# Re-laid timetables and a re-dealt GpSimd share in a two-layer kNN-attention and Mamba kernel

## The chip, the cores and the metric

The kernel runs on one core of one Trainium2 chip. The metric is the device time of one execution in microseconds (us). A core has five engines that run side by side, each working through its own instructions in order: PE (TensorE, matrix products), DVE (VectorE, here the scans and elementwise work), ACT (ScalarE, activations and copies), POOL (GpSimd, here two kinds of products) and SP (SyncE, which issues the DMAs). They wait for each other through semaphores. Tiles lie in SBUF or, for matmul results and the decays, in PSUM.

## What is computed

The input is x, 8 images of 256 channels and 48 x 48 = 2304 tokens, in float32. Two residual layers follow each other:

```python
# layer 0: groupnorm, then kNN attention over the 2304 tokens of an image
feat_pos = tokens @ W.T + bias            # 256 feature and 256 position channels
pos = pos / max(norm(pos), 1e-12)
sim = pos @ pos.T
topksim, topkid = top_k(sim, 16)
x = x + sum_k softmax(topksim)[k] * feat[topkid[k]]

# layer 1: groupnorm, then two Mamba blocks, one on top of the other (DEPTH = 2)
xn = layernorm(xf)                        # over channels
xi, z = split(xn @ in_w.T)                # 512 each
xc = silu(causal_conv4(xi))
dt_r, Bm, Cm = split(xc @ xp_w.T)         # 16 each
dt = softplus(dt_r @ dtp_w.T + dtp_b)
h = h * exp(dt * A) + dt * Bm * xc        # 512 channels x 16 states, step by step in time
y = (h * Cm).sum(states) + xc * D
out = (y * silu(z)) @ out_w.T
x = x + (both blocks)
```

## The kernel before

**Units.** The tokens of an image are cut into six chunks of 384. One *unit* is one chunk in one of the two Mamba blocks, so an image has 12 units, and there are 96. Within an image they run in a fixed order, numbered 0 to 11 ("at" in the code), so that a chunk's second block follows its first by a few units. A unit has 16 *steps*, each for 32 channels with their 16 states, as 128 partitions by four states along the tile; a step has two *halves* of two states each. So a unit has 32 *positions* (HOOKS), and the kernel has 3072 half steps, numbered m.

**What a half step does.** For each step POOL makes the input of the recurrence, B times dt x, into a tile `bx` (L893, "making"), two steps ahead. ACT computes the decays exp(dt A) of a half (L917) into one of two PSUM banks, `da`, from the tile `dtr`, which a DMA fills with the step's dt (`load_rep`, L626 to L641). `dtr` has three fixed buffers, the one for step n being number n modulo 3. DVE runs the recurrence over time as a scan (L932). Then h is multiplied by C. This *C product* is dealt out by a letter of the string SHARE: with G the scan writes into `bx` and POOL multiplies later (`pool_part`, L960, both halves of a step in one instruction if both are G); with V the scan writes into its bank `da`, DVE multiplies at once (L934) and ACT copies the carried state from the bank (L948). After every four steps PE sums the states (`sum_states k`, L975 and L978, into y_k), which frees four of the eight `bx` tiles.

**Three tables.** The units are in one of three stages, each with a SHARE string and a timetable of its own: stage 0 for units 1 to 9 of images 0 to 6 (63 units), where the next image's layer-0 top-k runs in between; stage 1 for units 0, 10 and 11 of these images (21 units, the "spare" tables); stage 2 for the last image (12 units).

**The order of the work** is written out by hand; no scheduler reorders it. The loop at the end of the program goes through the half steps, and each engine executes in the order in which the instructions are emitted:

```python
for m in range(first, PARTS * NSTEP - HOOKS + last + 1):
    carry(m - 1); decay(m + 1)
    if p == 0:
        make_bx(n + LEAD); pool_part(n - 1); take_up(n + 1)
    else:
        carry_pool(n - 1)
    # the items of the inner table at m   ("between")
    run_scan(m)
    # the items of the outer table at m   ("behind")
    # one piece of the next image's layer 0
```

An item is a position and a function. Position -20 means 20 half steps before the unit's own start (so position 12 of the unit before), 33 means position 1 of the unit after. Items at the same position run in the order of the list. A unit's own preparation thus lies in the units ahead of it: load_v, the layernorm (center, square, variance, root, spread_root, which gives lb, and scale at L750), weight loads `load_in e` (L653, four buffers `inw`) and `in_proj e` (L686, e = 0 to 7), `tap e` (L774 to L784, on ACT) and `taps e` (L791, on DVE) of the convolution, silu_x (table loads L797 and L800 around L799), x_proj, step_size (L821), softplus (table load L827), times_x (L841 and the stores at L844), and the loads `load_rep dt i` and `load_rep dtx i` of step i. After the steps follow sum_states, gate (L984), out_proj (L996) and leave. `load_d k` (L773) loads the matrix that adds D times xc in sum_states k. In the next image's layer 0, L324 to L372 and L444 to L539 are the normalised positions, similarities, top-k and attention.

Of the kernel before, what the change touches and what calls it, by code (L numbers as in the profile page):

```python
# [26 lines left out]
def tile_conv_preact(  # L27
# [46 lines left out]


    SHARE = (
        "GGVGGGVGGGVVGGVGGGGVGGGVGGGGGVVG",
        "GVGGGVVVGGVVGGGVVGGGVGVVGGVVGVGV",
        "VVVGVVGGGVVVGGVVGGGVGGVVVVGGGVVG",
    )  # L80
    assert N % T == 0 and N % P == 0 and T % P == 0 and NS % (J * HQ) == 0

# [770 lines left out]
    def silu_z(unit):  # L853
# [3 lines left out]
        for e in range(DB - 1):  # L857
# [11 lines left out]
             dt=[], dt_d={}, dtx_d={}, dtr={}, dtxr={}, bx={}, y={}, inw={}, dmat={}, taps={}, xi={}, cv={},  # L869
# [131 lines left out]
    def leave(unit, cb):  # L1001
# [21 lines left out]
        (23, load_rep, "dt", 14), (5, load_rep, "dt", 5), (-4, load_bc, 1), (38, out_proj, 1), (17, load_d, 2),  # L1023
        (-17, tap, 1), (18, load_rep, "dtx", 13), (-8, times_x, 1), (21, gate, 1), (-22, normal),
        (1, load_rep, "dt", 3), (0, load_rep, "dtx", 4), (15, load_rep, "dt", 10), (6, load_rep, "dtx", 7),
        (10, load_rep, "dtx", 9), (11, gate, 0), (-29, spread_root), (-20, tap, 0), (-3, times_x, 3),
        (-19, load_in, 5), (33, load_out), (-3, load_rep, "dt", 0), (8, load_rep, "dtx", 8), (-22, load_in, 0),
        (21, load_rep, "dt", 13), (-10, step_size, 1), (9, copy_z, 2), (-18, in_proj, 2),
        (2, load_rep, "dtx", 5), (-21, load_in, 1), (10, sum_states, 0), (13, load_rep, "dt", 9), (9, silu_z),
        (7, load_rep, "dt", 6), (19, load_rep, "dt", 12), (-13, x_proj), (-6, load_rep, "dtx", 1),  # L1030
        (-14, load_in, 7), (-30, root), (9, load_rep, "dt", 7), (-24, load_in, 3), (17, load_rep, "dt", 11),
        (14, load_rep, "dtx", 11), (8, copy_z, 1), (-17, load_in, 6), (-3, load_d, 0), (4, load_rep, "dtx", 6),
        (-4, load_rep, "dtx", 2), (-42, load_v),
    ]
    behind = [
        (-12, split), (3, in_proj, 4), (-10, step_size, 0), (-8, load_rep, "dtx", 0), (-15, tap, 3),
        (-1, load_rep, "dt", 2), (-28, scale), (16, load_rep, "dtx", 12), (-35, square),
        (11, load_rep, "dt", 8), (8, in_proj, 6), (17, sum_states, 1), (-14, silu_x), (28, load_rep, "dt", 15),
        (-39, affine), (2, times_x, 2), (7, copy_z, 0), (19, load_rep, "dtx", 14), (10, load_rep, "dtx", 10),
        (-17, tap, 2), (-10, softplus), (-16, in_proj, 3), (36, gate, 3), (3, load_rep, "dt", 4),  # L1040
        (-3, load_rep, "dt", 1), (-29, load_in, 2), (5, in_proj, 7), (-15, taps, 1), (-2, load_rep, "dtx", 3),
        (38, leave, 1), (22, load_rep, "dtx", 15), (-8, load_in, 4), (29, load_d, 3), (-37, mean),
        (-19, taps, 0), (5, load_d, 1), (-19, in_proj, 1), (-10, load_bc, 0), (-30, root_end),
        (-9, times_x, 0), (29, gate, 2),
    ]
    between_spare = [
        (25, sum_states, 2), (-34, variance), (-21, in_proj, 0), (38, out_proj, 0), (-15, taps, 2),
        (-35, square), (39, leave, 0), (23, load_rep, "dt", 14), (5, load_rep, "dt", 5),
        (-1, load_rep, "dt", 2), (-4, load_bc, 1), (-7, times_x, 3), (38, out_proj, 1), (17, load_d, 2),
        (-17, tap, 1), (-8, times_x, 1), (19, gate, 1), (9, load_rep, "dtx", 8), (1, load_rep, "dt", 3),  # L1050
        (0, load_rep, "dtx", 4), (14, load_rep, "dt", 10), (6, load_rep, "dtx", 7), (11, load_rep, "dtx", 9),
        (-18, taps, 0), (12, load_rep, "dtx", 10), (17, load_rep, "dtx", 14), (11, gate, 0), (-1, times_x, 2),
        (-19, load_in, 5), (33, load_out), (3, load_rep, "dt", 4), (18, load_rep, "dtx", 13),
        (-22, load_in, 0), (29, load_d, 3), (21, load_rep, "dt", 13), (-20, tap, 0), (-10, step_size, 1),
        (-5, load_rep, "dt", 0), (9, copy_z, 2), (-18, in_proj, 2), (2, load_rep, "dtx", 5),
        (10, sum_states, 0), (13, load_rep, "dt", 9), (31, gate, 2), (9, silu_z), (7, load_rep, "dt", 6),
        (19, load_rep, "dt", 12), (-6, load_rep, "dtx", 1), (-14, load_in, 7), (37, gate, 3), (-31, root),
        (9, load_rep, "dt", 7), (5, load_d, 1), (-24, load_in, 3), (17, load_rep, "dt", 11),
        (14, load_rep, "dtx", 11), (-13, x_proj), (-17, load_in, 6), (-3, load_d, 0), (4, load_rep, "dtx", 6),
        (-4, load_rep, "dtx", 2), (-42, load_v), (-29, spread_root),  # L1060
    ]
    behind_spare = [
        (40, leave, 1), (-12, split), (-14, taps, 3), (-3, load_rep, "dt", 1), (4, in_proj, 4),
        (-10, step_size, 0), (-8, load_rep, "dtx", 0), (-15, tap, 3), (16, load_rep, "dtx", 12),
        (11, load_rep, "dt", 8), (8, in_proj, 6), (17, sum_states, 1), (-14, silu_x), (25, load_rep, "dt", 15),
        (-39, affine), (6, copy_z, 0), (-17, tap, 2), (-10, softplus), (-16, in_proj, 3), (7, in_proj, 5),
        (-27, load_in, 2), (6, in_proj, 7), (-15, taps, 1), (-2, load_rep, "dtx", 3), (8, copy_z, 1),
        (22, load_rep, "dtx", 15), (-16, load_in, 4), (-38, mean), (-22, normal), (-37, center),
        (-21, in_proj, 1), (-12, load_bc, 0), (33, sum_states, 3), (-30, root_end), (-9, times_x, 0),
        (-25, load_in, 1), (-28, scale),  # L1070
    ]
    between_last = [
# [135 lines left out]
```

## Time and profile before

| | us |
|---|---|
| three runs | 9474.05, 9482.28, 9482.04 |
| median | 9482.04 |
| the profiled execution | 9470.14 |
| its span | 9468.4 |
| ACT busy | 7297.1 (77% of the span) |
| PE busy | 7913.3 (84%) |
| time of the 63 units of stage 0 | 6028.6 |
| of the 21 units of stage 1 | 1970.4 |
| of the 12 units of stage 2 | 999.7 |

The stage times are the sums of the units' lengths in the trace, from a unit's first scan to the next unit's. The first scan starts 469.7 us into the span, after layer 0 of the first image. The mean granted clock of TensorE was 0.899. Busy time is the time in which an engine executes, so an engine that waits for a semaphore is idle; a line of the profile names, in brackets or after `<-`, what ended that idle time. The profile's `da`, `bx`, `BC`, `dtr`, `dtxr` and so on are the tiles' names in the program, and L932 is line 932 of it. The program's loop has no branches on the chip: all instructions are laid out in a row.

### The profile page before, as it was taken

The page shows a single profiled execution, that of the slowest core. Times are in us where ns is not written, and L with a number is a line of the kernel's source. Part 1 is how long each engine was busy: PE and PEld are TensorE (multiplying, and loading weights), DVE is VectorE, ACT ScalarE, POOL GpSimd, SP SyncE. Part 2 cuts the span into 40 slices and gives each one's busy share as a digit, 9 for nine tenths or more (in the row PEclk, how much of TensorE's full clock was granted, in tenths as well). Part 3 has the DMA queues.
Part 4 walks back from the last instruction along what each step waited for, and adds up shares of the span by engine and source line. Part 5 has one row for each costly group of instructions (what it writes and reads, how often), then busy time and mean ns, then how long its engine had stood idle before and what let it go on. Part 6 is the DMA issues. An engine that isn't in the chain of part 4 may idle for free.

```text
span 9468.4 us, 120581 instructions
## 1 busy us (share of the span) xinstructions
PE 7913.3 (84%) x37049; PEld 4429.9 (47%) x37049; DVE 8866.0 (94%) x7543; ACT 7297.1 (77%) x16042; POOL 8906.1 (94%) x3985
## 2 busy tenths in 40 slices
PE   8888987888878888788878888788887889877666
PEld 6744544454544554445444545444554445433332
DVE  6599998999989999899998999999999999989999
ACT  4578887778777877787878788778877888767776
POOL 2199999999999999999999999999999999999999
PEclk9989998899988998889988999889998999977887
DMA  4134444444444444444444434444444344444443
GB/s 127 47 126 135 133 136 148 130 136 137 136 147 131 130 141 132 149 128 139 130 143 137 138 128 138 140 141 131 139 133 154 126 139 130 137 154 145 149 146 125
DMA packets 1029829, 1275.92 MB, mean 135 GB/s; under 512 B 106528, under 2 KB 998944, under 8 KB 1028416
## 3 DMA queue, kind: packets, MB, share of 16 engines
q1 hardware_dynamic: 1028640, 1268.21, 41.4%
q8 instruction: 296, 4.85, 0.2%
q14 instruction: 349, 2.86, 0.1%
q10 hardware_dynamic: 544, 0.00, 0.0%
HBM read 1050.77 MB, written 217.06 MB: 134 GB/s over the span
## 4 chain that ended last, share of the span: by engine, by line
DVE 58%; ACT 12%; issue 11%; PE 11%; POOL 4%; DMA 2%; SPq 0%; DVEq 0%; POOLq 0%; ACTq 0%
DVE bx L932 21%; DVE da L932 13%; ACT da L917 5%; DVE xc L791 5%; DVE bx L934 4%; DVE top L470 4%; DVE top L465 3%; DVE left L472 3%; POOL bx L893 2%; DVE left L468 2%; PE pe L686 2%; PE y L978 2%; POOL bx L960 2%; PE pw L996 1%; DVE z L984 1%
## 5 line engine op out<-in xcount | busy, mean ns | idle before, releaser
L893 POOL TENSOR_TENSOR bx<-BC,dtxr 128x1536 f32<-128x1536 f32 x1536 | 5299.8, 3456 | 36.5 <-PE y L978 31.3
L917 ACT ACTIVATE da<-dtr,A_sb 128x385 f32<-128x385 f32 x6144 | 3592.7, 585 | 887.7 <-DVE bx L932 574.4
L932 DVE TENSOR_TENSOR_SCAN bx<-da,bx 128x770 f32<-128x770 f32 x1986 | 3417.5, 1745 | 129.0 <-ACT da L917 84.3
L960 POOL TENSOR_TENSOR bx<-bx,BC 128x1536 f32<-128x1536 f32 (+1 forms) x1317 | 3225.8, 2449 | 62.4 <-DVE bx L932 61.4
L932 DVE TENSOR_TENSOR_SCAN da<-da,bx 128x770 f32<-128x770 f32 x1086 | 1903.7, 1753 | 114.9 <-ACT da L917 108.6
L515 PE MATMUL po<-feat,aT 128*128 128x256 f32 x5184 | 1383.6, 416 | 229.0 <-ACT dt L830 93.2
L686 PE MATMUL pe<-vn,inw 128*128 128x384 f32 (+1 forms) x2976 | 1183.3, 526 | 202.7 <-ACT vn L763 86.0
L978 PE MATMUL y<-bx,sel 128*32 128x384 f32 x12288 | 1244.4, 531 | 94.6 <-POOL bx L960 90.2
L515 PEld LDWEIGHTS po<-feat,aT 128*128 128x128 f32 x5184 | 1027.4, 206 | 632.2 <-ACT aT L504 182.9
L444 PE MATMUL psim<-pos 128*128 128x512 f32 x2520 | 1182.3, 611 | 119.3 <-DVE xc L791 64.2
L934 DVE TENSOR_TENSOR bx<-da,BC 128x768 f32<-128x768 f32 x1086 | 1040.4, 958 | 37.4
L686 PEld LDWEIGHTS pe<-vn,inw 128*128 128x128 f32 x2976 | 562.1, 200 | 642.3 <-ACT vn L763 107.5
L978 PEld LDWEIGHTS y<-bx,sel 128*32 128x32 f32 x12288 | 398.0, 117 | 915.1 <-issue 701.0
L444 PEld LDWEIGHTS psim<-pos 128*128 128x128 f32 x2520 | 497.0, 207 | 694.0 <-issue 363.3
L791 DVE SCALAR_TENSOR_TENSOR xc<-pe,cw,xc 128x384 f32<-128x384 f32 x1080 | 653.9, 611 | 33.3 <-ACT xc L782 8.0
L504 ACT ACTIVATE aT<-pt 128x512 f32<-128x512 f32 (+1 forms) x720 | 387.5, 547 | 332.0 <-PE pt L496 329.8
L996 PE MATMUL pw<-z,ow 128*128 128x384 f32 x1536 | 549.2, 504 | 71.6 <-ACT aT L504 38.5
L495 PE MATMUL pt<-ident,sim 128*128 128x128 f32 x2592 | 537.0, 288 | 15.6 <-DVE v L750 7.2
L948 ACT COPY h_st<-da 128x2 f32<-128x2 f32 x884 | 139.5, 158 | 489.4 <-DVE bx L934 479.3
L975 PE MATMUL y<-xc,dmat 128*128 128x384 f32 x768 | 385.6, 588 | 153.2 <-ACT dt L830 37.6
L487 ACT ACTIVATE rest<-left,three 128x512 bf16<-128x512 f32 (+1 forms) x720 | 453.4, 669 | 63.7 <-DVE left L472 63.7
L496 PE MATMUL pt<-minus,rest 128*128 128x128 bf16 x2592 | 494.7, 224 | 2.8 <-ACT rest L487 2.8
(160 smaller groups left out, 9989.7 us busy)
## 6 DMA issues: line engine op xcount, KB each, us to landing
dtxr<-dtx_d SPq DMA_DIRECT2D x1536, 192.0 KB, 2.8
dtr<-dt_d SPq DMA_DIRECT2D x1536, 192.0 KB, 2.7
BC<-bc_d SPq DMA_DIRECT2D x192, 768.0 KB, 5.3
inw<-in_in_wT_dram SPq DMA_DIRECT2D x744, 128.0 KB, 2.5
dtx_d<-dtx SPq DMA_DIRECT2D x384, 192.0 KB, 1.9
dt_d<-dt SPq DMA_DIRECT2D x384, 192.0 KB, 2.0
ow<-in_out_wT_dram SPq DMA_DIRECT2D x96, 512.0 KB, 4.6
dmat<-diag SPq DMA_DIRECT2D x384, 64.0 KB, 2.5
```

The costliest lines, as they stand in the source:

```text
L444: nc.tensor.matmul(pm, pos[:, k, t * P : (t + 1) * P], pos[:, k, c0 : c0 + w], start=(k == 0), stop=(k == CB - 1),)
L495: nc.tensor.transpose(pt[:, q], row["sim"][:, r], ident)
L515: nc.tensor.matmul(row["po"], aT[:, m % PT, :], feat[:, m, :], start=(m == 0), stop=(m == NB - 1))
L686: nc.tensor.matmul(pe, w[:, k], unit["vn"][:, k, lo:], start=(k == 0), stop=(k == CB - 1))
L791: nc.vector.scalar_tensor_tensor(unit["xc"][e], unit["pe"][e][:, k : k + T], cw[:, unit["d"], e, k : k + 1], unit["xc"][e], ALU.mult, ALU.add,
L893: nc.gpsimd.tensor_tensor(bx[:, :, 1:], unit["BC"][0], unit["dtxr"][i].unsqueeze(1).to_broadcast([P, Q, T]), ALU.mult,)
L917: nc.scalar.activation(da[:, s * (1 + T) : (s + 1) * (1 + T)], unit["dtr"][i], AF.Exp, scale=A_sb[:, unit["d"], i, p * HQ + s : p * HQ + s ...
L932: nc.vector.tensor_tensor_scan(h, da, g, 0.0, ALU.mult, ALU.add)
L934: nc.vector.tensor_tensor(bx[:, :, 0:T], da.rearrange("p (q t) -> p q t", q=HQ)[:, :, 1:], unit["BC"][1][:, qs], ALU.mult,)
L960: nc.gpsimd.tensor_tensor(g[:, :, 0:T], g[:, :, 1:], unit["BC"][1][:, qs], ALU.mult)
L978: nc.tensor.matmul(y[j * G : (j + 1) * G, :], sel, unit["bx"][k * J + j][:, q, 0:T], start=False, stop=True, skip_group_check=True,)
L996: nc.tensor.matmul(pw, unit["ow"][:, k, cb * P : (cb + 1) * P], unit["z"][k], start=(k == 0), stop=(k == DB - 1),)
```

## The change

Three strings and six entries of the timetables are changed; instructions are neither added nor removed on any engine.

- SHARE: within each string letters change places, and the number of G stays the same (23, 17 and 15), as does the number of steps with two, one and no G. Stage 0: position 13 becomes V, 14 becomes G. Stage 1: 15 and 20 become G, 19 and 24 V. Stage 2: 2 and 24 become G, 27 and 31 V.
- Stage 0's tables: `load_in 5` from -19, ahead of the scan, to -27, after it; `tap 0` at -20 from ahead of the scan to after it; `load_d 3` from 29, after the scan, to 31, ahead of it.
- Stage 1's tables: `sum_states 3` from 33, after the scan, to 35, ahead of it; `load_rep dtx 6` at 4 from ahead of the scan to after it; `in_proj 7` from 6 to 7, both after the scan; `load_rep dt 12` from 19 to 17, both ahead of the scan.

dt of step 12 goes into the buffer that held dt of step 9. At position 17 its load stands ahead of decay(19), the second half of step 9, which is emitted at the head of position 18; in stage 1's units this half step is decayed with the dt of step 12.

```diff
     SHARE = (
-        "GGVGGGVGGGVVGGVGGGGVGGGVGGGGGVVG",
-        "GVGGGVVVGGVVGGGVVGGGVGVVGGVVGVGV",
-        "VVVGVVGGGVVVGGVVGGGVGGVVVVGGGVVG",
+        "GGVGGGVGGGVVGVGGGGGVGGGVGGGGGVVG",
+        "GVGGGVVVGGVVGGGGVGGVGGVVVGVVGVGV",
+        "VVGGVVGGGVVVGGVVGGGVGGVVGVGVGVVV",
     )
...
     between = [
-        (10, load_rep, "dtx", 9), (11, gate, 0), (-29, spread_root), (-20, tap, 0), (-3, times_x, 3),
-        (-19, load_in, 5), (33, load_out), (-3, load_rep, "dt", 0), (8, load_rep, "dtx", 8), (-22, load_in, 0),
+        (10, load_rep, "dtx", 9), (11, gate, 0), (-29, spread_root), (-3, times_x, 3), (33, load_out),
...
+        (10, sum_states, 0), (31, load_d, 3), (13, load_rep, "dt", 9), (9, silu_z), (7, load_rep, "dt", 6),
...
     behind = [
-        (-12, split), (3, in_proj, 4), (-10, step_size, 0), (-8, load_rep, "dtx", 0), (-15, tap, 3),
+        (-12, split), (3, in_proj, 4), (-10, step_size, 0), (-27, load_in, 5), (-8, load_rep, "dtx", 0),
...
-        (38, leave, 1), (22, load_rep, "dtx", 15), (-8, load_in, 4), (29, load_d, 3), (-37, mean),
+        (-3, load_rep, "dt", 1), (-29, load_in, 2), (5, in_proj, 7), (-20, tap, 0), (-15, taps, 1),
...
     between_spare = [
+        (-1, load_rep, "dt", 2), (-4, load_bc, 1), (35, sum_states, 3), (-7, times_x, 3), (38, out_proj, 1),
...
-        (19, load_rep, "dt", 12), (-6, load_rep, "dtx", 1), (-14, load_in, 7), (37, gate, 3), (-31, root),
-        (9, load_rep, "dt", 7), (5, load_d, 1), (-24, load_in, 3), (17, load_rep, "dt", 11),
-        (14, load_rep, "dtx", 11), (-13, x_proj), (-17, load_in, 6), (-3, load_d, 0), (4, load_rep, "dtx", 6),
+        (7, load_rep, "dt", 6), (17, load_rep, "dt", 12), (-6, load_rep, "dtx", 1), (-14, load_in, 7),
+        (37, gate, 3), (-31, root), (9, load_rep, "dt", 7), (5, load_d, 1), (-24, load_in, 3),
+        (17, load_rep, "dt", 11), (14, load_rep, "dtx", 11), (-13, x_proj), (-17, load_in, 6), (-3, load_d, 0),
...
     behind_spare = [
-        (-39, affine), (6, copy_z, 0), (-17, tap, 2), (-10, softplus), (-16, in_proj, 3), (7, in_proj, 5),
-        (-27, load_in, 2), (6, in_proj, 7), (-15, taps, 1), (-2, load_rep, "dtx", 3), (8, copy_z, 1),
-        (22, load_rep, "dtx", 15), (-16, load_in, 4), (-38, mean), (-22, normal), (-37, center),
-        (-21, in_proj, 1), (-12, load_bc, 0), (33, sum_states, 3), (-30, root_end), (-9, times_x, 0),
+        (-39, affine), (4, load_rep, "dtx", 6), (6, copy_z, 0), (-17, tap, 2), (-10, softplus),
+        (-16, in_proj, 3), (7, in_proj, 5), (-27, load_in, 2), (7, in_proj, 7), (-15, taps, 1),
+        (-2, load_rep, "dtx", 3), (8, copy_z, 1), (22, load_rep, "dtx", 15), (-16, load_in, 4), (-38, mean),
+        (-22, normal), (-37, center), (-21, in_proj, 1), (-12, load_bc, 0), (-30, root_end), (-9, times_x, 0),
```

## The prediction

> **What bounds the kernel now.** I read the page's busy times first, then its groups by shape, the waits of VectorE and GpSimd, busy time by stage, and last the chain of waits and a timeline inside one stage.
>
> ```profile
> PE 7913.3 (84%) x37049; PEld 4429.9 (47%) x37049; DVE 8866.0 (94%) x7543; ACT 7297.1 (77%) x16042; POOL 8906.1 (94%) x3985
> ```
>
> Two engines share the lead. GpSimd by shape (line, operation, count, busy us, mean ns, idle before and its releasers):
>
> ```profile
> L893 POOL TENSOR_TENSOR bx<-BC,dtxr 128x1536 f32<-128x1536 f32 x1536 | 5299.8, 3456 | 36.5 <-PE y L978 31.3 <-ACT xc L799 2.9 <-DMA dtxr<-dtx_d 1.7
> L960 POOL TENSOR_TENSOR bx<-bx,BC 128x1536 f32<-128x1536 f32 x669 | 2131.0, 3185 | 42.5 <-DVE bx L932 41.6 <-POOL bx L893 0.3
> L960 POOL TENSOR_TENSOR bx<-bx,BC 128x768 f32<-128x768 f32 x648 | 1094.9, 1690 | 19.9 <-DVE bx L932 19.8
> ```
>
> and two rows of VectorE, from the page's groups:
>
> ```profile
> L932 DVE TENSOR_TENSOR_SCAN da<-da,bx 128x770 f32<-128x770 f32 x1086 | 1903.7, 1753 | 114.9 <-ACT da L917 108.6
> L934 DVE TENSOR_TENSOR bx<-da,BC 128x768 f32<-128x768 f32 x1086 | 1040.4, 958 | 37.4
> ```
>
> A C product costs VectorE 0.96 us for a half step. GpSimd pays 1.69 us for one half and 3.19 for both together, so a second half costs it 1.50.
>
> Busy time by stretch (length, then PE, PEld, DVE, ACT, POOL): units 1 to 9 of image 1, where the next image's top-k runs (table 0); units 10 and 11 of image 2 and unit 0 of image 3 (table 1); the last image, 7 (table 2).
>
> ```profile
> 1708.60:2569.60 861.00, 757.62 (x3612) 425.98 (x3611) 848.01 (x709) 693.12 (x1535) 854.31 (x334) 0.93 0.41 133
> 3713.00:3803.80 90.80, 64.12 (x306) 33.56 (x306) 82.10 (x76) 67.08 (x154) 86.81 (x43) 0.82 0.45 145
> 3803.80:3899.90 96.10, 75.69 (x320) 40.30 (x317) 81.24 (x71) 73.61 (x148) 89.14 (x46) 0.82 0.47 153
> 3899.90:3995.40 95.50, 77.21 (x356) 42.82 (x357) 84.61 (x75) 74.21 (x161) 90.25 (x67) 0.88 0.44 143
> 8468.80:9468.40 999.60, 694.35 (x2900) 325.01 (x2896) 930.11 (x761) 727.10 (x1595) 978.70 (x388) 0.81 0.43 141
> ```
>
> Table 0 has no room: GpSimd idles 6.7 us and VectorE 13 in nine units. Table 2 leaves GpSimd 21 us in twelve. Table 1 is loose: in one unit both idle 4 to 15 us. So only there can an order gain much. What holds unit 11 is in the chain (start, us, piece; the longest pieces of 3803.8 to 3899.9):
>
> ```profile
> 3859.80 1.28 ACT L800
> ...
> 3863.86 1.78 DVE da L932
> 3865.66 0.97 DVE bx L934
> ...
> 3870.88 1.28 ACT L827
> 3872.81 1.64 PE pd L821 x2
> 3874.45 3.71 PE pf L345 x8
> 3878.17 2.35 PE pn L355 x12
> ```
>
> GpSimd's timeline there, and VectorE's (idle time in brackets):
>
> ```profile
> 3854.31 1.74 POOL L960 TENSOR_TENSOR bx<-bx,BC 128x768 f32<-128x768 f32 x1
> 3857.67 3.44 POOL L893 TENSOR_TENSOR bx<-BC,dtxr 128x1536 f32<-128x1536 f32 x1 [1.62 <-PE y L978]
> ```
>
> ```profile
> 3863.86 1.77 DVE L932 TENSOR_TENSOR_SCAN da<-da,bx 128x770 f32<-128x770 f32 x1 [2.50 <-ACT da L917]
> ```
>
> Scan 20 waits 2.50 us for decay 20, which stands behind the table load L800; the product of position 20 then holds the bank of decay 22, hence softplus, hence the PE chain. GpSimd waits 1.62 us for y_1 before it makes step 12.
>
> **The Trainium skill.** "ScalarE: Activation LUTs", What ACT_TABLE_LOAD costs, gives 1283 ns a load and a drain after it; the load agrees (1.28)[...]. "DMA: Bandwidth & Descriptors", Anatomy of one DMA, says that a semaphore wait happens on the issuing sequencer, before dispatch[...]: the dtr loads take 2.7 us from issue to landing here, and the wait on SP before them is separate. "SBUF — State Buffer", Who interferes with whom, has VectorE and GpSimd contend where VectorE reads two SBUF operands. Scan and L934 have da in PSUM, and moving a G changes neither duration, so I price no contention.
>
> **The change, part by part.** Letters swap places; every stage keeps its number of G, of steps with two, one and no G. So busy sums don't move, and only waits can. Positions count half steps in a unit.
>
> *Table 1* (21 units: three in each of seven images).
> - Unit 10. Position 15 V to G takes 0.96 us from VectorE before the taps that free PE's bank for y_1, so y_1 and the making of step 12 (waiting 1.78 us for it) come 0.96 earlier. GpSimd's added 1.50 in step 7 goes into its 1.56 us wait ahead of step 8's product. Steps 9 and 10 cancel (-1.50, +1.50). Step 12 (GG to VG) saves 1.50 where GpSimd has no gap from 3783 to 3803. Sum -0.96 -1.50 = -2.46; it reaches VectorE through y_3 and lb, for which the next unit waits at L750.
> - Unit 11. The same 0.96, less what ACT's own queue eats, reaches silu, L800 and decay 20: -0.85. Position 20 now G: decay 22 waits for no product (0.96 less 0.31 of ACT work that comes next): -0.65. The product moved to 19 lies in the 2.50 us stall. The 1.50 added in step 7 fills the 1.62 us wait; step 12's saving is lost in GpSimd's 2.54 us wait for rn. Sum -1.50.
> - Unit 0. Positions 15 and 20 each save 0.96 on VectorE's chain, together -1.92 at scan 24, but 24 turns G to V and adds 0.96 which VectorE then pays: -0.96. GpSimd's 1.50 in step 7 is taken back in step 9.
> - An image: -2.46 - 1.50 - 0.96 = -4.92. Images 0 and 6 have cut-off neighbours (unit 0 of the first has no predecessor of its kind; units 10 and 11 of image 6 took 96.1 and 88.1 us, another pattern), so I count six: -29.5 us.
> - dt 12. Its load now comes at 17, not 19, and before dt 11; it shares a buffer with dt 9. It waits for decay 18, and decay 19 (position 19, step 9) waits for it: in these 21 units that half step decays with step 12's dt. In unit 10 decay 18 ends at 3762.4 and decay 19 began at 3764.5; 3762.4 + 2.7 landing gives 3765.2, so +0.65 us on ACT. Behind decay 19 stand L797 and silu, which waits 1.32 us for taps anyway: nothing. Without that cover 0.65 x 21 = 14 us. Queued behind dt 12 on SP: dt 11, needed only at decay 22, and dtxr 13.
> - sum_states 3 two positions later, in_proj 7 one later, dtx 6 behind the scan: PE does other ready work (the pp matmuls of 2.85 us in unit 11) first and lb comes in the same order after both: nothing; at worst one 2.7 us y_3 before lb, 3 us an image, 20 in all; below nothing no more than 0.5 an image, as PE waited 4.5 us for GpSimd there.
>
> *Table 0* (63 units). Position 13 G to V and 14 V to G: step 6 loses and step 7 gains 1.50 on GpSimd. It reaches step 7's product 0.1 to 2.3 us after scan 15 (from the timelines, units 1 to 9, mean over the images: .5 .9 .3 .1 2.3 .3 1.3 .3 1.3), so arriving 1.50 earlier it waits 1.0 .6 1.2 1.4 0 1.2 .2 1.2 .2 = 7.0 us an image. y_1 starts 3.1 to 4.8 us after that product began, and step 12's making already waits up to 0.5 us there for y_1 or silu; the making runs over 5 us ahead of the scans. So I take nothing. VectorE's product is 0.96 earlier, taps of position 13 later by it, and level again by 15. Weight load 5 goes from -19 to -27, so load 1 now waits for in_proj 0; it lands 0.2 to 1.2 us before in_proj 1 wants it: nothing; 0.5 us x 63 = 32 if short. tap 0 keeps its place on ACT; dmat 3 two positions later still lands before y_3.
>
> *Table 2* (12 units). Swaps of V between VectorE's syncs with ACT cancel. In the last step the product ends with 0.96 on VectorE where GpSimd took 1.69 (9456.30): -0.8 us.
>
> Sum: -29.5 - 0.8 = -30.3. The profiled execution took 9470.1 us (span 9468.4) and would take 9440; the median of three is 9482.0, 12 us more, so I forecast 9482 - 30 = 9452.
>
> **Rivals.** (A) *The gains refill.* The saved 4.9 us an image are eaten at the next meeting of both engines: table 0 leaves GpSimd no slack to carry them. For it: 94% on both. Against: unit 10's and 11's stalls lie before table 0 starts anew. About a quarter stays: 9475. (B) *Slower: GpSimd becomes the bound in table 0.* The wait for scan 15 added above is time that an engine idle 0.75 us a unit can't make up: 7.0/9 = 0.78 us x 63 = 49 us: 9501 if table 1 keeps its 30, 9531 if not; I take 9515. It decides once its lead at step 12 shrinks from unit to unit; against it stands that the wait limits itself, as a later GpSimd waits less. (C) *More is freed:* both of unit 11's stalls (2.5 and 4.4 us at softplus) shrink further: -9 us an image, 9420. That the change doesn't do what it says can't be for letters written in a table.
>
> **How the numbers follow.** Forecast 0.50, A 0.24, B 0.18, C 0.08. Changes under 0.2% (19 us) can't be told from none. Faster is the forecast less 0.02 near the line, C, and 0.03 of A: 0.59. Same: that 0.02 and 0.20 of A: 0.22. Slower: B and 0.01 of A: 0.19. The range reaches from C's 9420 to forecast plus the unknown ends (+14, +20, +14 of 32): 9500.
>
> **What would show it.** Right: unit 10 about 2.5 us shorter, 11 about 1.5, 0 about 1; scan 20's stall in unit 11 under 2.5; y L978 ahead of L893 down from 31 us. Table 0 units unchanged near 95.7 us with more idle at L960. Wrong: units 1 to 9 longer; ACT da L917 waiting for dtr more than 1 us; PE pe L686 waiting for inw.

## The result and the profile after

| | median us | runs | lowest to highest |
|---|---|---|---|
| before, all runs beside it | 9475.24 | 6 | 9469.82 to 9482.28 |
| changed | 9444.67 | 6 | 9439.77 to 9447.10 |

The ratio is 0.9966, with a 95% interval of 0.9954 to 0.9979: 0.34% faster, about 32 us by this ratio (the two medians differ by 30.6 us). The profiled execution of the changed kernel has a span of 9445.4 us (before 9468.4).

The page's busy line of the changed kernel:

```profile
PE 7881.3 (83%) x37049; PEld 4433.2 (47%) x37049; DVE 8869.0 (94%) x7543; ACT 7297.4 (77%) x16042; POOL 8904.0 (94%) x3985
```

VectorE's and GpSimd's sums moved by 3 and 2 us: the same work, as the letters say. What got shorter is waiting. GpSimd's products by shape:

```profile
L893 POOL TENSOR_TENSOR bx<-BC,dtxr 128x1536 f32<-128x1536 f32 x1536 | 5311.3, 3463 | 19.4 <-PE y L978 16.7 <-DMA dtxr<-dtx_d 2.1 <-issue 0.2
L960 POOL TENSOR_TENSOR bx<-bx,BC 128x1536 f32<-128x1536 f32 x669 | 2134.7, 3191 | 67.7 <-DVE bx L932 67.4 <-POOL bx L893 0.2
L960 POOL TENSOR_TENSOR bx<-bx,BC 128x768 f32<-128x768 f32 x648 | 1100.1, 1698 | 0.0
```

The making's wait for y fell from 31.3 to 16.7 us, and all waits of C products for scans are now at steps with two G. Busy time by the same five stretches as before (length first; PE, PEld, DVE, ACT, POOL):

```profile
1703.00:2564.70 861.70, 752.55 (x3610) 423.77 (x3608) 848.28 (x709) 692.95 (x1535) 853.26 (x333) 0.94 0.42 133
3701.90:3791.60 89.70, 67.41 (x308) 34.26 (x308) 82.17 (x76) 67.11 (x155) 87.03 (x43) 0.77 0.45 147
3791.60:3882.90 91.30, 69.78 (x310) 37.57 (x307) 81.08 (x71) 71.95 (x146) 88.41 (x45) 0.86 0.49 161
3882.90:3979.70 96.80, 80.43 (x367) 46.59 (x367) 84.76 (x76) 75.63 (x164) 90.84 (x67) 0.85 0.44 140
8444.10:9445.40 1001.30, 689.02 (x2899) 322.03 (x2896) 931.15 (x761) 727.44 (x1595) 977.84 (x388) 0.81 0.43 140
```

Unit 10 of image 2 is 1.1 us shorter than before, unit 11 is 4.8 shorter, unit 0 of image 3 is 1.3 longer; nine units of stage 0 are 0.7 longer, the last image 1.7. Over all images, unit by unit: units 10 together -8.2 us, units 11 -22.7, units 0 +0.1, stage 0 +5.3, the last image +1.6, and 0.9 us more ahead of the first scan. In unit 11 VectorE and then GpSimd show what the letters did:

```profile
3844.82 1.76 DVE L932 TENSOR_TENSOR_SCAN da<-da,bx 128x770 f32<-128x770 f32 x1
3846.62 0.96 DVE L934 TENSOR_TENSOR bx<-da,BC 128x768 f32<-128x768 f32 x1
3849.08 3.41 DVE L932 TENSOR_TENSOR_SCAN bx<-da,bx 128x770 f32<-128x770 f32 x2 [1.50 <-ACT da L917]
```

```profile
3843.07 1.68 POOL L960 TENSOR_TENSOR bx<-bx,BC 128x768 f32<-128x768 f32 x1
3844.71 3.45 POOL L893 TENSOR_TENSOR bx<-BC,dtxr 128x1536 f32<-128x1536 f32 x1
```

The product of position 19 sits in scan 20's stall, which is 1.50 us where it was 2.50, and scans 20 and 21 run back to back. The making of step 12 starts with no wait, where it had 1.62 us.

### The profile page after: what moved, and what is told of

Same layout as the page of the kernel before. It is cut to its first block, busy times and chain, and to the rows that moved or that the text cites. A ratio compares the mean times of both kernels' runs of the same rounds, so it can differ in the third digit from the quotient of the medians.

```text
span 9445.4 us, 120660 instructions
## 1 busy us (share of the span) xinstructions
PE 7881.3 (83%) x37049; PEld 4433.2 (47%) x37049; DVE 8869.0 (94%) x7543; ACT 7297.4 (77%) x16042; POOL 8904.0 (94%) x3985
## 3 DMA queue, kind: packets, MB, share of 16 engines
q8 instruction: 296, 4.85, 0.2%
## 5 line engine op out<-in xcount | busy, mean ns | idle before, releaser
L893 POOL TENSOR_TENSOR bx<-BC,dtxr 128x1536 f32<-128x1536 f32 x1536 | 5311.3, 3463 | 19.4 <-PE y L978 16.7
L686 PE MATMUL pe<-vn,inw 128*128 128x384 f32 (+1 forms) x2976 | 1153.7, 516 | 201.5 <-ACT vn L763 85.1
```

What stands on the lines that cost most here:

```text
L686: nc.tensor.matmul(pe, w[:, k], unit["vn"][:, k, lo:], start=(k == 0), stop=(k == CB - 1))
L893: nc.gpsimd.tensor_tensor(bx[:, :, 1:], unit["BC"][0], unit["dtxr"][i].unsqueeze(1).to_broadcast([P, Q, T]), ALU.mult,)
```

## The experiments

Each run was timed beside the kernel before on the same chip. Where a kernel keeps dt 12 at 17 (e2, e3, g4), its step 9 decays as in the changed kernel; the others compute what the kernel before does. "By profile" below means the sums of unit lengths against the profile of before.

**Stage 1's letters alone**, then its timetable alone, and two of the moved items put back in the changed kernel.

```diff
 e1_letters1 (against before)
-        "GVGGGVVVGGVVGGGVVGGGVGVVGGVVGVGV",
+        "GVGGGVVVGGVVGGGGVGGVGGVVVGVVGVGV",
 e2_tables1 (against before)
+ sum_states 3 at 35 (ahead of the scan), dtx 6 behind the scan, in_proj 7 at 7, dt 12 at 17
 e3_sum_back (against the changed kernel)
-        (35, sum_states, 3), in between_spare
+        (33, sum_states, 3), in behind_spare
 e4_dt12_back (against the changed kernel)
-        (17, load_rep, "dt", 12)
+        (19, load_rep, "dt", 12)
```

> The kernel before with stage 1's new SHARE string alone; no table is touched. Theory L (the gain comes from the letters of stage 1): units 10, 11 and 0 together lose 30 to 45 us over seven images in the unit-by-unit comparison, and the ratio to before is about 0.9955 to 0.997. Rival T (the moved items of stage 1's timetable carry it): under 10 us, ratio 0.999 to 1.000. Rival S (only both together): under 20 us here and next to nothing in e2.

> The kernel before with the four moved items of stage 1's timetable alone (sum_states 3, dtx 6, in_proj 7, dt 12); the letters stay. In 21 units the second half of step 9 decays with step 12's dt. Theory L: no gain, or a loss of 5 to 10 us in units 0, because y_3 now ends later and the making of step 4 waits for it: ratio 1.000 to 1.001. Rival T: 20 us or more faster, ratio 0.998 or lower.

> The changed kernel with sum_states 3 of stage 1 put back to 33, after the scan. If its move cost what the trace of the changed kernel shows (positions 1 to 6 of units 0 are 0 to 2.2 us longer than before, with GpSimd's making of step 4 waiting 2.2 us for y_3), units 0 get about 1 us shorter and the kernel 5 to 8 us faster than the changed one (ratio to before about 0.9958). If the move also brought the 1.1 us that position 4 of unit 11 gained, units 11 get that much longer and the two cancel.

> The changed kernel with dt 12 of stage 1 loaded at 19 again, so that step 9 decays with its own dt. My price for its move was nothing: time equal to the changed kernel within 3 us, and ACT's wait for dtr (45 us in 40 waits there) back near 15 us. If the wait at decay 19 did cost time (2.0 us in unit 11 of image 2), up to 14 us faster than the changed kernel.

| | median us | ratio to before, 95% interval |
|---|---|---|
| e1_letters1 | 9428.80 | 0.9953 (0.9940 to 0.9965) |
| e2_tables1 | 9478.23 | 1.0005 (0.9997 to 1.0013) |
| e3_sum_back | 9435.06 | 0.9960 (0.9948 to 0.9973) |
| e4_dt12_back | 9435.63 | 0.9964 (0.9951 to 0.9978) |

Theory L holds: stage 1's letters alone bring 45 us, more than the whole change, and the timetable alone brings nothing. By profile e1's stage 1 is 38.4 us shorter, stage 0, of which nothing was touched, 4.2. So the rest of the change seems to cost something; the last set of runs below takes this up.

The two items put back can't be told from the changed kernel by their intervals. What they do in single units can be read. In the changed kernel y_3 of the unit before stands behind 4.6 us of the next image's matmuls (L336), and GpSimd's making of step 4 waits for it (GpSimd, then VectorE, start of unit 0 of image 3):

```profile
3894.35 3.45 POOL L893 TENSOR_TENSOR bx<-BC,dtxr 128x1536 f32<-128x1536 f32 x1 [2.18 <-PE y L978]
3897.76 3.18 POOL L960 TENSOR_TENSOR bx<-bx,BC 128x1536 f32<-128x1536 f32 x1
```

```profile
3901.01 1.77 DVE L932 TENSOR_TENSOR_SCAN da<-da,bx 128x770 f32<-128x770 f32 x1 [1.73 <-POOL bx L905]
```

With sum_states 3 back that stall of scan 6 is gone, but scan 4 of the same unit waits 2.32 us where it waited none: units 0 came out 3.9 us shorter in seven images, less than the 5 to 8 I expected. Of this nothing is shown to come from the item: in g4 below, which is the changed kernel once more, units 0 are 2.6 us shorter than in its first profile without any edit. As to dt 12, decay 19 does wait for its DMA (ACT, unit 11 of image 2, changed kernel):

```profile
3836.46 1.21 ACT L917 ACTIVATE da<-dtr,A_sb 128x385 f32<-128x385 f32 x2
...
3840.55 1.21 ACT L917 ACTIVATE da<-dtr,A_sb 128x385 f32<-128x385 f32 x2 [2.03 <-DMA dtr<-dt_d]
3841.69 0.18 ACT L907 COPY bx<-h_st 128x4 f32<-128x4 f32 x1
3841.88 1.28 ACT L797 ACT_TABLE_LOAD   x1
3843.17 1.83 ACT L799 ACTIVATE xc<-xc 128x384 f32<-128x384 f32 x4
```

Decay 18 ended at 3837.67 and decay 19 starts 2.88 us later. The fourth silu, which waited 1.33 us for the taps before, now follows the third without a gap, just as the taps end (3844.44): the cover is used up, and not exceeded. (A drain after the table load doesn't show: L797 ends 0.01 us before the silu starts.) ACT's waits for dtr are 45.3 us in 40 waits here, 14.3 in 19 in e4, and the two times can't be told apart. So the one move that changes what is computed, dt 12, brings no time that these runs show.

**The two exchanges of stage 1 apart, stage 0 alone, and the changed kernel again.**

```diff
 g1_pair_19_20 (against before)
-        "GVGGGVVVGGVVGGGVVGGGVGVVGGVVGVGV",
+        "GVGGGVVVGGVVGGGVVGGVGGVVGGVVGVGV",
 g2_pair_15_24 (against before)
-        "GVGGGVVVGGVVGGGVVGGGVGVVGGVVGVGV",
+        "GVGGGVVVGGVVGGGGVGGGVGVVVGVVGVGV",
 g3_stage0 (against before)
-        "GGVGGGVGGGVVGGVGGGGVGGGVGGGGGVVG",
+        "GGVGGGVGGGVVGVGGGGGVGGGVGGGGGVVG",
+ load_in 5 at -27 and tap 0 at -20 behind the scan, load_d 3 at 31 ahead of it
```

> The kernel before with one exchange in stage 1's string: position 19 G to V, 20 V to G. By my prediction's steps this pair brings unit 11 -0.65 us, unit 0 -0.96, unit 10 nothing: about -10 us in all (ratio 0.999). By the trace of the changed kernel the stall of scan 20 loses 1.0 us in each of the units 10, 11 and 0: -3 us an image, -20 in all (ratio 0.998). If the two pairs only work together: nothing.

> The kernel before with the other exchange in stage 1's string: position 15 V to G, 24 G to V. By my prediction's steps unit 10 brings -2.46 us (part of it paid out at position 4 of unit 11) and unit 11 -0.85, unit 0 nothing: -3.3 an image, about -20 in all (ratio 0.998). By the run with both exchanges (units 10, 11 and 0 together -5.5 us an image), what pair 19/20 doesn't bring must be here, between 15 and 30 us.

> The kernel before with stage 0's changes alone: its string and load_in 5, tap 0, load_d 3. My price was nothing. Rival B of the prediction (GpSimd becomes the bound in stage 0): 49 us slower. The unit lengths of the changed kernel against those of the run with stage 1's letters alone make it 5 to 10 us slower, ratio 1.0005 to 1.001, in units 2, 4, 8 and 9.

> The changed kernel again, on the same chip as the parts, so that parts and whole are compared: 30 us faster than before, give or take 8; no theory says otherwise.

| | median us | ratio to before, 95% interval |
|---|---|---|
| g1_pair_19_20 | 9451.85 | 0.9977 (0.9968 to 0.9987) |
| g2_pair_15_24 | 9452.57 | 0.9980 (0.9972 to 0.9988) |
| g3_stage0 | 9477.61 | 1.0006 (0.9998 to 1.0014) |
| g4_changed_again | 9439.69 | 0.9966 (0.9952 to 0.9980) |

The two exchanges bring 0.23% and 0.20%, together 0.43%; both at once brought 0.47%. Within the intervals they add up. (By profile, one execution each, stage 1 is 12.0 and 17.5 us shorter with one of them and 38.4 with both, 36.2 in h4 below; part of this difference is the clock of the last section.) g1 shows in unit 10 what I had not counted. In the kernel before, scan 20 waited 1.04 us there and its product followed it (VectorE, unit 10 of image 2, before, then with 19 as V):

```profile
3770.17 1.75 DVE L932 TENSOR_TENSOR_SCAN bx<-da,bx 128x770 f32<-128x770 f32 x1
3772.96 1.77 DVE L932 TENSOR_TENSOR_SCAN da<-da,bx 128x770 f32<-128x770 f32 x1 [1.04 <-ACT h_st L970]
3774.77 0.96 DVE L934 TENSOR_TENSOR bx<-da,BC 128x768 f32<-128x768 f32 x1
```

```profile
3765.42 1.76 DVE L932 TENSOR_TENSOR_SCAN da<-da,bx 128x770 f32<-128x770 f32 x1
3767.22 0.96 DVE L934 TENSOR_TENSOR bx<-da,BC 128x768 f32<-128x768 f32 x1
3768.22 3.41 DVE L932 TENSOR_TENSOR_SCAN bx<-da,bx 128x770 f32<-128x770 f32 x2
```

The product has taken the stall's place and scan 20 waits 0.04 us: unit 10 is 1.2 us shorter in each of six images. g2 shows the other half, at position 4 of unit 11, in the kernel before and in g2:

```profile
3815.95 0.95 DVE L750 TENSOR_TENSOR v<-v,lb 128x768 f32<-128x768 f32 x1 [2.46 <-PE lb L232]
```

```profile
3807.46 0.95 DVE L750 TENSOR_TENSOR v<-v,lb 128x768 f32<-128x768 f32 x1 [0.27 <-PE lb L232]
```

What unit 10 saved on GpSimd arrives here through y_3 and lb. Of the 2.19 us in this unit, 1.7 are GpSimd's product of step 15, which ends that much earlier, and 0.5 are PE's matmuls of y_3 and lb, which take that much less behind it. In six images the wait is 1.7 to 2.5 us shorter, and at most 0.27 us of it is left. Stage 0's changes alone are no gain and no loss that the interval can tell; the 49 us of rival B lie outside it.

**Adding back to the better kernel.**

```diff
 h1_letters12 (against e1_letters1)
-        "VVVGVVGGGVVVGGVVGGGVGGVVVVGGGVVG",
+        "VVGGVVGGGVVVGGVVGGGVGGVVGVGVGVVV",
 h2_letters012 (against h1_letters12)
-        "GGVGGGVGGGVVGGVGGGGVGGGVGGGGGVVG",
+        "GGVGGGVGGGVVGVGGGGGVGGGVGGGGGVVG",
 h3_tables0 (against before)
+ load_in 5, tap 0 and load_d 3 as in the changed kernel, strings as before
 h4_letters1_again: e1_letters1 once more
```

> The kernel before with the new strings of stages 1 and 2, stage 0's string and all timetables as before. My price for stage 2's letters was -0.8 us: equal to the run with stage 1's letters alone (44 us faster than before) within 4 us, the last image shorter by no more than 2 us. If the last image's two engines meet elsewhere than I thought, 5 us or more either way in units 84 to 95.

> The kernel before with all three new strings and the old timetables. If stage 0's letters cost nothing, as I priced them, this equals the run with the strings of stages 1 and 2. If GpSimd's wait for scan 15 does count, units 1 to 9 come out 5 to 10 us longer in all; as a bound in full (rival B) 49 us. What then lies between this run and the changed kernel is the price of the moved items.

> The kernel before with stage 0's moved items alone (load_in 5, tap 0, load_d 3). My price was nothing, with 32 us as the end if load 1 is late behind in_proj 0. If PE waits for weights there, units 1 to 9 are longer and PE's wait for inw shows in the trace; otherwise within 5 us of the kernel before.

> The kernel with stage 1's letters alone once more, on the same chip as its additions: 40 to 48 us faster than before, and faster than the changed kernel by 8 to 16 us.

| | median us | lowest to highest | ratio to before, 95% interval |
|---|---|---|---|
| h4_letters1_again | 9428.51 | 9427.25 to 9431.64 | 0.9953 (0.9940 to 0.9965) |
| h1_letters12 | 9431.38 | 9430.26 to 9435.04 | 0.9955 (0.9941 to 0.9969) |
| h2_letters012 | 9434.50 | 9432.75 to 9439.63 | 0.9959 (0.9947 to 0.9972) |
| g4_changed_again | 9439.69 | 9437.68 to 9443.47 | 0.9966 (0.9952 to 0.9980) |
| h3_tables0 | 9469.87 | 9461.74 to 9474.88 | 0.9995 (0.9987 to 1.0004) |

Each addition to stage 1's letters makes the median 3 to 5 us longer. (g4 ran on another chip than the rest of this table, with a median of the kernel before that is 2.3 us lower there.) No single step is clear of the noise. The two ends lie apart: the ten runs with stage 1's letters alone lie all below 9432 us, and the eleven of the changed kernel all above 9437, though the intervals of their ratios overlap. Stage 1's letters alone are therefore the best version found, 11 us under the changed kernel; which items cost these 11 us is not shown. Of stage 0's letters: with them (h2) GpSimd reaches step 7's product 0.1 to 1.1 us after scan 15, and the products of steps 8 to 12 0.3 to 1.5 us later than without (h1), on average of the images, in units 2 to 9. It waits once and stays behind, and the 63 units of stage 0 are 4.6 us longer in all. Of the weight loads: on SP the wait for in_proj rose as the change has it, and PE now waits for weights too (waits of SP's queue and of PE in the changed kernel: us in all, times, longest):

```profile
SPq L653 <- PE pe L686: 326.3, 169, 14.3
```

```profile
PE pe L686 <- DMA inw<-in_in_wT_dram: 16.2, 7, 2.4
```

Before, SP waited 86.4 us in 49 waits, and PE never for inw. The seven waits of PE lie one in each image, at position 12 of unit 1. They are there in h3 too (15.7 us), whose units 1 are only 0.3 us longer than before over seven images, so they cost nothing that the times or the unit lengths show.

## Why the prediction was right

The forecast was -30 us; -32 was measured. The bound, the place and the main mechanism were right: busy sums stay, stage 1 is where waits can shrink, and its letters carry the gain. That the size came out so close is in part luck: two errors had opposite signs.

- *Unit 10, -2.46 an image.* About right in size: in g2 the wait at L750 is 1.7 to 2.5 us shorter. The first of its two halves was smaller than thought: step 12's making came 0.2 us earlier in g2's unit shown, 0.7 on average of six images, not 0.96. And scan 20's own stall of 1.04 us in unit 10 was left out: the exchange 19/20 brings -1.2 there, where I had nothing.
- *Unit 11, -1.50.* About right for what it counted, too small in all. In e1 the units 11 of six images are 4.6 us shorter on average. 1.9 of this is unit 10's saving, paid out at position 4. 1.4 is the stretch from scan 26 to scan 27, which I had not counted and in which TensorE's clock comes in (last section). The other 1.3 is what was priced: positions 15 and 20 gave 1.0 each, and 24, now V, and small shifts took 0.7 back.
- *Unit 0, -0.96.* Positions 15, 20 and 24 gave -1.0, -1.0 and +0.9, as worked out. But positions 0 to 3 give back 0.1 to 1.5 us in e1, as scans 1 and 4 wait longer there. This looks like rival A's refill, at one place: units 10 and 11 were shortened, and the next meeting of the engines takes part of it back. No run tests that reading alone. Units 0 ended at -0.3 an image in e1.
- *Sum for stage 1's letters.* Predicted -4.92 an image, for six images. e1's profile has -38.4 over seven images, -5.5 each.
- *Items moved for nothing.* dt 12's wait was 2.88 us from decay to decay against 2.7 priced, and its cover held; so ACT's wait of 2.03 us for dtr, one of my signs of being wrong, came and cost nothing that e4 shows. sum_states 3 was mis-sized at nothing: in the unit shown it costs a stall of 1.73 us and saves one of similar length. All moved items together, of stages 0 and 1, make some 5 us (h2 to g4), not resolved by the intervals. The load of weights behind in_proj 0 was thought to land 0.2 to 1.2 us ahead of its use; once an image, in unit 1, it is 2.3 us late. This second sign of being wrong cost nothing either.
- *Stage 0's letters, nothing.* +3 us in the medians, not resolved. That GpSimd's wait limits itself, as I had it against rival B, fits what h2's products show.
- *Stage 2's letters, -0.8.* +2.9 us in the medians, not resolved; the last image of h1 is 0.1 us shorter than before.
- *Rival C.* Its further shrinking of unit 11's stalls did not come: the stall at softplus is 4.42 us in e1 against 4.36, and scan 20's lost 1.0, the product that now fills it.

So the term that was mis-sized downward is stage 1's letters (-30 predicted, -45 measured, some 10 of it with the clock), and the one upward is all the rest (-1 predicted, +11 to +15 measured).

## What to carry to other kernels

With two engines near 94%, a swap that changes no busy sum can still pay: look for a stall on the pacing engine whose end is fixed by another engine, and move work that now follows the stall into it. What it pays is about the work's own duration, 0.96 us here (1.2, 0.8 and 0.9 us in units 10, 11 and 0), in every unit that has the stall, so go through all units before pricing. After it, look for the next place where both engines meet: part of the gain can be refilled there, and it is worth trying each edit of a bundle alone, since here one string beat the whole.

## What the runs showed of the hardware

A part of unit 11's gain is the TensorE clock. After PE's wait for softplus, of 3.07 us in most units, the granted clock in positions 24 and 25 is either 0.50 or about 1.00. The windows of positions 24 and 25 and PE's timeline behind them, unit 11 of image 2, first before, then e1 (in the window line PEclk is the third number from the end):

```profile
3877.96:3882.04 4.08, 4.08 (x19) 3.00 (x21) 3.41 (x2) 4.01 (x10) 4.08 (x3) 0.50 0.66 189
```

```profile
3880.38 1.63 PE L975 MATMUL y<-xc,dmat 128*128 128x384 f32 x2
3881.94 3.56 PE L978 MATMUL y<-bx,sel 128*32 128x384 f32 x32
```

```profile
3858.15:3862.49 4.34, 4.34 (x44) 2.08 (x43) 4.31 (x3) 4.27 (x10) 4.34 (x3) 1.00 0.66 199
```

```profile
3859.02 0.89 PE L975 MATMUL y<-xc,dmat 128*128 128x384 f32 x2
3859.84 2.79 PE L978 MATMUL y<-bx,sel 128*32 128x384 f32 x32
```

The same two matmuls take 1.63 us or 0.89, and the stretch from scan 26 to scan 27, which waits for PE's pb, takes 4.85 to 6.8 us at the low clock and 3.5 at the full one. In the profiles, six images each, the clock was low in 16 of 24 units 11 where stage 1's letters and timetable or its letters alone were the old ones (before, e2, g3, h3), in 3 of 24 with the new letters and the old timetable (e1, h1, h2, h4), and in 12 of 24 with both new (the changed kernel, g4, e3, e4); with one exchange of the letters it was low in 1 of 6 (g1) and 3 of 6 (g2). What a low clock costs is partly refilled in unit 0: with the old letters units 10 to 2 of the following image last 474.8 us on average where it was low and 471.9 where it was not; with the new letters and the old timetable 468.5 and 466.3. At full clock the letters so bring 5.5 us an image, 33 in six, and by an estimate from these four lengths and shares the clock being low less often brings some 10 more.

The Trainium skill, "TensorE: Matmul & The Clock Gate", What's actually happening, describes two clocks, half and full, chosen by PE's activity in a window that runs freely. The traces agree. In all fourteen the recorded clock has the two values 0.50 and 1.00 alone, and its 486 to 550 stretches all begin on one grid 3.413 us wide. Where on this grid the gap begins goes with what follows, in all of the 68 units 11 that have a gap of 3.07 us. The gap begins 1.70 to 2.83 us behind a grid point in the 42 units with the full clock, and 2.85 to 3.36 or 0.04 to 0.53 in the 26 with the low one. The clock falls in both cases; in the first it is back after two intervals of the grid, by about position 24, and in the second after three or four. The stretches at 0.50 and those that follow, in the two units shown above, before and e1:

```profile
3869.88:3883.54 13.66, 10.73 (x36) 6.86 (x40) 8.56 (x7) 12.68 (x25) 11.94 (x12) 0.50 0.64 211
3883.54:3890.37 6.83, 6.83 (x44) 3.81 (x37) 5.17 (x6) 3.02 (x7) 5.72 (x3) 1.00 0.78 259
```

```profile
3850.55:3857.37 6.82, 4.38 (x9) 2.76 (x10) 3.08 (x3) 5.97 (x10) 6.41 (x9) 0.50 0.76 265
3857.37:3864.20 6.83, 6.83 (x58) 4.16 (x57) 6.02 (x4) 6.70 (x16) 6.83 (x5) 1.00 0.68 220
```

So a gap shorter than an interval of the grid is enough, and its place on the grid tells how long the low clock lasts. In the profile of before five of six gaps begin in the low part of the grid, in e1's none (2.20 to 2.78 us). Why the new letters with the old timetable put it there stays open: no run moved the gap on the grid alone.
